# Equal blocks of nine neighbour chunks, and another order of the set-up, in a sparse four-layer graph network

## The chip, the cores and the metric

The kernel runs on one core of a Trainium2 chip. The metric is the device time of one execution in microseconds; lower is better. The engines named below are TensorE (PE; its weight loads are listed apart as PEld), VectorE (DVE), ScalarE (ACT), GpSimd (POOL) and SyncE (SP, which only issues DMAs). [...]

## The reference

Sixteen graphs with 1024 nodes of 128 features share one 1024 x 1024 adjacency matrix with about 8 edges per node. Four layers follow one another: graph transformer, graph attention, graph transformer, graph transformer.

```python
def _L0_gnn_ref(adj_matrix, h, Wq, Wk, Wv, Wo, bo, ln1_g, ln1_b, W1, b1, W2, b2, ln2_g, ln2_b):
    ...
    scores = jnp.einsum('bnhd,bmhd->bhnm', Q, K) / jnp.sqrt(jnp.asarray(HEAD_DIM, jnp.float32))
    mask = (adj_matrix == 0)[None, None, :, :]
    scores = jnp.where(mask, -jnp.inf, scores)
    attn = jax.nn.softmax(scores, axis=-1)
    attn_out = jnp.einsum('bhnm,bmhd->bnhd', attn, V).reshape(B, N, OUT_DIM)
    x = h + (attn_out @ Wo + bo)
    x = _layer_norm(x, ln1_g, ln1_b)
    y = jax.nn.relu(x @ W1 + b1) @ W2 + b2
    x = _layer_norm(x + y, ln2_g, ln2_b)
    return x

def _L1_gnn_ref(x, adj, W, a_src, a_dst, ln_gamma, ln_beta):
    h = x @ W
    e = (h @ a_src)[:, :, None] + (h @ a_dst)[:, None, :]
    e = jnp.where(e >= 0, e, NEG_SLOPE * e)
    e = jnp.where(adj[None, :, :] == 0, -jnp.inf, e)
    ...
    y = jnp.einsum('bij,bjd->bid', att, h) + x
```

Everything is fp32, with 8 heads of 16 features.

## The kernel before

Only existing edges are computed. The kernel sorts the nodes by degree, so that nodes with like numbers of neighbours stand together, and gathers each neighbour's key and value rows from a table in DRAM.

**Blocks and chunks.** The sorted nodes make eight rows of 128, each of four quarters of 32 nodes. A block of 128 nodes takes one quarter from each of four rows: `ROWS` (L55) says which, and `CAPS` (L61) how many neighbour slots each of the four quarters gets. Four slots of one quarter (4 x 32) fill one chunk of 128 gathered rows; the leftover slots of the four quarters share one mixed chunk. A chunk is one indirect DMA on POOL (L955). Before the change blocks have 11, 9, 9, 9, 9, 9, 9 and 7 chunks. `PIECES` (L92) puts chunks together in pairs, with the mixed chunk alone as the fourth piece, so a nine-chunk block has five pieces, an eleven-chunk one six, a seven-chunk one four. In an attention layer each piece is a part. In the graph attention layer, neighbouring pieces are merged to parts of up to four chunks.

**Order of units.** The 16 graphs form two groups of eight. A unit is one block of one group in one layer; units run layer by layer, group 0's eight blocks and then group 1's. For each part the main loop does: `products` on DVE (L967, gathered keys times queries), `exponentials` (a reduction on DVE, L990, and the exponential on ACT, L994), `weighted` on DVE (L1018, values times weights), then `summed` on PE (L1034, summing slots per node by 0/1 marks). When a unit's last part is summed, `divided` takes a reciprocal on DVE (L1071) and starts two tails, one for each half of the graphs: output projection, layer norms, feed-forward, and the next layer's projections to its table. Gathers run four parts ahead.

**What is put between.** After each of these steps `others()` issues a bit of the other work: pieces of the two tails ("a" and "b") and of the next unit's queries ("q"). In an attention layer it goes by a written list, `PLANS` (L834), of fifteen entries; a part has three openings for it, so five parts have fifteen. Where a block ends with entries still to do, the closing loop issues them at once (L1254). At the end of a unit all that is left in `fronts` is issued in a row (L1273).

**Set-up.** `graph` loads the adjacency matrix (`edges`, three buffers), counts degrees (L263), broadcasts a sort key through PE (`over_partitions`), ranks the nodes (L309), and turns ranks into node numbers (`node_i`, L366). Then it gathers the adjacency rows in sorted order (`by_position`, POOL) and makes for each row of 128 nodes the list of its neighbours, by repeated max-of-8 and match-replace passes on DVE (L402 to L410). A list as long as the row's largest cap, rounded up to 8, needs that many passes. `slots` spreads the lists to slots of a block: matmuls on PE, then `idx` and `marks` on DVE (L444 to L460). Beside it, `at_once(0)` projects group 0's input into the first table (PE L644, L573; ACT; table writes on SP). The generator `graph` yields numbers, which are steps of that projection to be issued, and words, on which the driver at L1169 issues other work: "load" for the first unit's input, "spread" and "slots" for the two halves of the first block's slots, "queries" for its queries. Group 1's input is projected by `at_leisure(1)` (the list `slow`) after the set-up, in steps between the parts of layer 0, and must be done before group 1's first gather.

Of the kernel before, what the change touches and what calls it, by code (L numbers as in the profile page):

```python
# [18 lines left out]
ALU = mybir.AluOpType  # L19
# [4 lines left out]
D = 128  # L24
# [19 lines left out]
T = N // P  # L44
# [7 lines left out]
S = 4  # L52
J = P // 32

ROWS = (  # L55
    (0, 1, 2, 3, 4, 5, 7, 6),
    (7, 6, 3, 5, 2, 1, 0, 4),
    (7, 6, 5, 1, 2, 0, 3, 4),
    (1, 0, 2, 3, 4, 7, 5, 6),
)  # L60
CAPS = (  # L61
    (24, 5, 4, 11), (12, 6, 6, 12), (10, 9, 8, 9), (9, 8, 11, 8),
    (8, 10, 10, 8), (7, 12, 13, 4), (5, 14, 9, 8), (6, 8, 8, 6),
)
TOP = max(map(max, CAPS))
QUADS = TOP // S
MIX = J


def row_of(t, j):  # L70
    return ROWS[j][t]
# [62 lines left out]
AHEAD = 4  # L134
# [11 lines left out]
def sparse_path(ctx: ExitStack, tc: tile.TileContext, a: dict, out: bass.AP, flag):  # L146


    nc = tc.nc
# [9 lines left out]
    ident = const.tile([P, P], F32, name="ident")  # L159
    make_identity(nc, ident)  # L160

    centre = const.tile([P, P], F32, name="centre")
    nc.vector.tensor_scalar(centre, ident, 1.0 / D, None, ALU.subtract)

    rep = const.tile([P, J, S, 32], F32, name="rep")
    nc.gpsimd.memset(rep, 0.0)
    for j in range(J):
        q = slice(32 * j, 32 * j + 32)
        nc.vector.tensor_copy(
            rep[q, j], ident[q, q].rearrange("p (o n) -> p o n", o=1).to_broadcast([32, S, 32])  # L170
        )

    def rep_of(j, whole=False):
        q = slice(0, P) if whole else slice(32 * j, 32 * j + 32)
# [41 lines left out]
    at = [0]  # L216
# [17 lines left out]
    def graph(wide):  # L234
# [54 lines left out]
        def over_partitions(col):  # L289

            ps = bank([T, P])
            nc.tensor.transpose(ps, col, ident)
            turn = s1.tile([T, P], F32, tag="turn", name="turn")
            nc.vector.tensor_copy(turn, ps)
            dst = accs.tile([P, HF, GH * D], F32, tag="acc", name="acc")
            dst = dst.rearrange("p h d -> p (h d)")
            for t in range(T):
                nc.tensor.matmul(
                    dst[:, t * P : (t + 1) * P], sel[:, t, :], turn, start=True, stop=True
                )  # L300
            return dst
# [2 lines left out]
        key = s1.tile([P, T], F32, name="key")  # L304
        nc.vector.scalar_tensor_tensor(key, deg, float(N), nid, ALU.mult, ALU.subtract)
        keys = over_partitions(key)
        rank = s1.tile([P, T], F32, name="rank")
        for t in range(T):
            nc.vector.tensor_scalar(  # L309
# [31 lines left out]
        for t in range(T):  # L341
# [13 lines left out]
            if t == 0:  # L355
                spread = over_partitions(pack)
# [17 lines left out]


        order = sorted({row_of(0, j) for j in range(J)})
        order += [q for q in range(T) if q not in order]
        ahead = [by_position(q) for q in order[:3]]
        there = s1.tile([P, T], F32, name="there")
        for j in range(J):  # L380
            rows = slice(32 * j, 32 * j + 32)
            for t in range(T):
                q = row_of(t, j)
# [13 lines left out]
        nc.vector.tensor_tensor(bad, bad, low, ALU.add)  # L397
        yield 2

        for at, q in enumerate(order):  # L400
            v = vs[:, :N]
            nc.vector.scalar_tensor_tensor(v, ahead[at], 0.0, values, ALU.not_equal, ALU.mult)  # L402
            if at + 3 < T:
                ahead.append(by_position(order[at + 3]))
            top = -(-max(SORTED_CAPS[q * J : (q + 1) * J]) // 8) * 8
            for k in range(0, top, 8):
                nc.vector.max(lists[:, q, k : k + 8], v)
                if k + 8 < top:
                    last, v = v, vs[:, N:] if k % 16 == 0 else vs[:, :N]
                    nc.vector.match_replace(v, lists[:, q, k : k + 8], last, 0.0)  # L410
                yield 1
            if 0 < at < 5:
                yield ("load", "spread", "queries", "slots")[at - 1]

    def slots():

# [367 lines left out]
    def at_leisure(g):  # L784
        def fetch(k):
            rows = ones_.tile([P, GH, D], F32, tag=("xg", "xh")[k % 2], name="xg")
            if k < T * HF:
                nc.sync.dma_start(
                    rows.rearrange("p g d -> p (g d)"),
                    a["x"][k // HF * P : (k // HF + 1) * P, columns(g, k % HF)],  # L790
                )
            return rows

        ahead = [fetch(0), fetch(1)]
        yield
        for k in range(T * HF):
            steps = natural(g, k // HF, k % HF, ahead.pop(0))
            held[0] = True
            next(steps)
            ahead.append(fetch(k + 2))  # L800
            yield
            yield from steps
            held[0] = False
            if wanted[0]:
                yield
# [59 lines left out]
    def loaded(u):  # L865

        if u >= len(units):
            return
        l, g, t = units[u]
        xs[units[u]] = inputs.tile([P, HF, GH, P], F32, tag="x", name="x")  # L870
        if l == 0:
            x = xs[units[u]]
            nc.gpsimd.indirect_dma_start(
                out=x.rearrange("p h g d -> p (h g d)"), out_offset=None,
                in_=a["x"].rearrange("n (k c) -> (n k) c", k=GR),
                in_offset=bass.IndirectOffsetOnAxis(ap=places[:, g, t : t + 1], axis=0),
            )
            for h in range(HF):
                yield "idle"
                yield "idle"  # L880
                yield
                turned(x[:, h], x[:, h])
            yield
            return
        nc.sync.dma_start(
            xs[units[u]].rearrange("p h g n -> p (h g n)"),
            kept[l, g][t].rearrange("p h c -> p (h c)"),
        )
# [203 lines left out]
    slow = []  # L1092
# [3 lines left out]
    def advance(gens):  # L1096
        for gen in list(gens):
            got = next(gen, "end")
            if got == "end":
                gens.remove(gen)  # L1100
            elif got == "free":
                free.append(gen)
# [58 lines left out]
    with tc.manual_schedule():  # L1161
        wide = [gather_buffer() for _ in range(EDGES)]
        setup, entry, weights = graph(wide), at_once(0), load_weights("L0")
# [2 lines left out]
        next(entry)  # L1166
        more = [weights, load_graph_weights()]
        rest = slots()
        for i, room in enumerate(setup):  # L1169
            if i == T:  # L1170
                for gen in more:
                    next(gen)
            if room == "load":
                for _ in loaded(0):
                    next(entry, None)
            elif room == "queries":
                for _ in entry:
                    pass
                for _ in queries(0):
                    pass  # L1180
            elif isinstance(room, str):
                next(rest)
            else:
                for _ in range(room):
                    next(entry, None)
        for _ in entry:
            pass
        scratch.close()
        prods = ctx.enter_context(tc.tile_pool(name="prods", bufs=4))
        smalls = ctx.enter_context(tc.tile_pool(name="smalls", bufs=3))  # L1190
        slow.append(at_leisure(1))
        second = loaded(1)
        next(second)
        for i in range(AHEAD - 1):
            gathered(i)
        nc.gpsimd.memset(wide[3], 0.0)
        gathered(AHEAD - 1)
        fronts.extend([islice(rest, WAIT + 2), second] + more)
# [519 lines left out]
```

## Time and profile before

| | us |
|---|---|
| median of 3 runs | 2179.24 (2172.41 to 2185.14) |
| the profiled execution, its own time | 2187.6 |
| its span in the profile | 2185.3 |
| DMA: bytes, mean rate | 636.09 MB, 291 GB/s |
| first table gather issued by POOL | 88.22 |
| first reciprocal that closes a block | 156.73 |
| last reciprocal that closes a block | 2144.77 |

The profile is that of one execution, so durations and the sums made from them are measured against 2187.6, not against the median. A row of the timeline gives the start, the busy time, engine, source line, operation and tiles, a count, and in brackets how long the engine had been idle and what ended the wait. A row of the stage table gives for a stretch of the span the busy time of each engine with the number of instructions, and then the clock granted to PE, the busy share of the DMA engines and their rate.

### The profile page before, as it was taken

How to read it: one execution, taken by the hardware profiler on the slowest of the kernel's cores; microseconds unless marked ns; L12 is line 12 of the kernel's file. 1: busy time of each engine (PE TensorE's matmuls, PEld its weight loads, DVE VectorE, ACT ScalarE, POOL GpSimd, SP SyncE). 2: the span in 40 equal slices, each digit the busy share in tenths (PEclk: the TensorE clock that was granted, in tenths of full speed). 3: DMA queues.
4: the chain of work that ended last, by engine and by line, in shares of the span. 5: the costliest groups of instructions: out<-in, count | busy, mean ns of one | idle time of the engine just before them, and what ended most of it. 6: DMA issues, size and time to landing. Idle time of an engine off the chain costs nothing.

```text
span 2185.3 us, 36956 instructions
## 1 busy us (share of the span) xinstructions
PE 1976.5 (90%) x13396; PEld 1245.4 (57%) x13396; DVE 1857.3 (85%) x1363; ACT 1524.6 (70%) x5041; POOL 1047.6 (48%) x699
## 2 busy tenths in 40 slices
PE   6689999999999989998999999999998899988986
PEld 5446666656655545554556655666655555555554
DVE  7897899699997566678999979999789898889993
ACT  3348888778887545555788786878867778677874
POOL 3343445354555577774445434444344545444540
PEclk8699999899999999999999999999999999999998
DMA  7898988789998799898998878999787878678860
GB/s 261 287 309 304 327 296 300 245 278 318 326 325 275 261 324 346 322 375 291 313 356 312 319 255 301 343 318 346 277 282 272 292 286 288 226 280 288 290 207 21
DMA packets 164703, 636.09 MB, mean 291 GB/s; under 512 B 34568, under 2 KB 37384, under 8 KB 116014
## 3 DMA queue, kind: packets, MB, share of 16 engines
q0 software_dynamic: 88720, 485.08, 62.1%
q1 hardware_dynamic: 75792, 148.57, 20.1%
q8 instruction: 107, 1.75, 0.3%
q14 instruction: 84, 0.69, 0.1%
HBM read 581.08 MB, written 92.34 MB: 308 GB/s over the span
## 4 chain that ended last, share of the span: by engine, by line
PE 55%; issue 15%; DVE 9%; ACT 8%; DMA 7%; POOL 5%; another core or an unknown queue 0%; POOLq 0%; DVEq 0%; ACTq 0%
PE acc L1034 13%; PE ps L644 6%; DMA e<-table,idx 6%; PE ps L728 6%; PE yps L742 6%; PE ps L919 5%; POOL e L955 4%; PE ps L573 4%; PE yps L718 3%; DVE pr L1018 3%; PE yps L717 3%; PE yps L746 3%; PE ps L910 2%; DVE pr L967 2%; DVE sc L990 2%
## 5 line engine op out<-in xcount | busy, mean ns | idle before, releaser
L955 POOL DMA_INDIRECT e<-table,idx x576 | 900.9, 1564 | 965.9 <-DVE pr L1018 757.4
L1018 DVE TENSOR_TENSOR pr<-e,ex 128x2048 f32<-128x2048 f32 (+1 forms) x320 | 662.0, 2078 | 68.3 <-ACT ex L994 45.4
L1034 PE MATMUL acc<-pr,marks 128*32 128x512 f32 x2624 | 506.0, 606 | 35.8 <-DVE o L1074 19.7
L967 DVE TENSOR_TENSOR pr<-e,qr 128x2048 f32<-128x2048 f32 x192 | 441.0, 2297 | 93.9 <-PE acc L1034 31.4
L990 DVE TENSOR_REDUCE sc<-pr 128x128 f32<-128x2048 f32 (+1 forms) x240 | 497.5, 2073 | 8.1
L621 ACT ACTIVATE z<-yps,root 128x128 f32<-128x128 f32 x888 | 313.2, 369 | 69.2 <-PE yps L746 46.1
L1034 PEld LDWEIGHTS acc<-pr,marks 128*32 128x32 f32 x2624 | 106.8, 110 | 292.1 <-issue 238.6
L742 PE MATMUL yps<-W,f 128*128 128x128 f32 x1520 | 253.2, 284 | 16.7 <-ACT f L737 16.7
L742 PEld LDWEIGHTS yps<-W,f 128*128 128x128 f32 x1520 | 203.3, 191 | 98.5 <-ACT f L737 59.4
L637 ACT ACTIVATE z<-yps,rstd 128x128 f32<-128x128 f32 x888 | 251.1, 367 | 1.6
L922 ACT COPY qr<-ps 128x512 f32<-128x512 f32 x384 | 203.3, 601 | 38.9 <-PE ps L919 35.4
L573 PE MATMUL ps<-Wkv,xT 128*128 128x256 f32 x768 | 202.8, 406 | 14.9 <-ACT xT L650 10.4
L577 ACT COPY kv<-ps 128x512 f32<-128x512 f32 x176 | 102.7, 589 | 158.6 <-PE ps L573 146.0
L737 ACT ACTIVATE f<-ps,b 128x512 f32<-128x512 f32 x190 | 130.3, 686 | 86.2 <-PE ps L728 83.9
L728 PE MATMUL ps<-x,W 128*128 128x512 f32 x384 | 186.7, 609 | 1.1 <-ACT x L652 1.1
L644 PE MATMUL ps<-ident,z 128*128 128x128 f32 x896 | 153.8, 286 | 37.5 <-ACT qr L922 17.7
L621 ACT ACTIVATION_READ_ACCUMULATOR z<-yps,root 128x1 f32 x888 | 185.8, 209 | 0.0
L573 PEld LDWEIGHTS ps<-Wkv,xT 128*128 128x128 f32 x768 | 144.0, 199 | 68.1 <-issue 15.6
L919 PE MATMUL ps<-q,rep 32*128 32x512 f32 x768 | 163.7, 681 | 19.5 <-ACT q L914 12.9
L644 PEld LDWEIGHTS ps<-ident,z 128*128 128x128 f32 x896 | 107.7, 142 | 88.2 <-ACT qr L922 40.0
L717 PE MATMUL yps<-Wo,oT 128*128 128x128 f32 x768 | 155.5, 285 | 2.6 <-issue 1.5
L718 PE MATMUL yps<-centre,x 128*128 128x128 f32 x768 | 154.5, 284 | 1.0 <-ACT x L713 0.2
(174 smaller groups left out, 2550.6 us busy)
## 6 DMA issues: line engine op xcount, KB each, us to landing
table<-kv SPq DMA_DIRECT2D x88, 512.0 KB
kept<-xT SPq DMA_DIRECT2D x96, 256.0 KB
x<-kept SPq DMA_DIRECT2D x48, 512.0 KB
qx<-qr SPq DMA_DIRECT2D x48, 256.0 KB
e<-table,idx POOLq DMA_INDIRECT x576
table<-kv SPq DMA_DIRECT2D x32, 256.0 KB
qx<-qr SPq DMA_DIRECT2D x18, 384.0 KB
qx<-qr SPq DMA_DIRECT2D x42, 128.0 KB
```

The lines of the kernel that those rows point to most:

```text
L573: nc.tensor.matmul(ps[:, k, :], x[:, i + k, :], w[LAYERS[l][0], "Wkv"], start=True, stop=True,)
L621: nc.scalar.activation(z[:, i, :], y[:, i, :], AF.Square, scale=D**-0.5, bias=root, accum_out=total[:, i : i + 1],)
L637: nc.scalar.activation(z[:, i, :], y[:, i, :], AF.Copy, scale=rstd[:, i : i + 1])
L644: nc.tensor.transpose(ps[:, i, :], z[:, i, :], ident)
L728: nc.tensor.matmul(ps, p["W1"][:, f * P : (f + 1) * P], x1.rearrange("p g n -> p (g n)"), start=True, stop=True,)
L742: nc.tensor.matmul(ps[:, i, :], f1[:, f, i * P : (i + 1) * P], p["W2"][:, f, :], start=(f == 0), stop=False,)
L919: nc.tensor.matmul(ps, rep_of(j), q[32 * j : 32 * j + 32], start=True, stop=True)
L955: nc.gpsimd.indirect_dma_start(out=es[i][:, k, :], out_offset=None, in_=tables[l, g][:, :], in_offset=bass.IndirectOffsetOnAxis(ap=idx[:, ...
L967: nc.vector.tensor_tensor(prs[i][0][:, :n, :], es[i][:, :n, :ROW], qx[u].rearrange("p (o c) -> p o c", o=1) if (MIX, 0) in piece else of_p ...
L990: nc.vector.tensor_reduce(sc[:, :n, :], prs[i][0][:, :n, :].rearrange("p k (a d) -> p k a d", d=HD), mybir.AxisListType.X, ALU.add,)
L1018: nc.vector.tensor_tensor(prs[i][k0 // 2][:, :m, :].rearrange("p k (a d) -> p k a d", d=d), es[i][:, k0 : k0 + m, base : base + ROW].rearr ...
L1034: nc.tensor.matmul(outs[32 * j : 32 * j + 32], marks[:, mark, :], rhss, start=(chunk == mine[0]), stop=(chunk == mine[-1]),)
```

## The change

The change gives every block 36 slots, and so nine chunks, by new tables `ROWS` and `CAPS`. The first block is made of sorted rows 1, 4 and 6, the row with the longest lists (row 0, 23 slots) goes to blocks 1, 4, 6 and 7. `TOP` is rounded up to a multiple of 8, which leaves it at 24.

In the set-up, the fill of `centre` and `rep` moves on DVE from the start to a function `constants()`, called after the sort key's broadcast. The order of words changes: the first unit's input gather is issued before the lists, the first half of the slots after the third list, the second half after the fourth list, followed by the first unit's input, its queries and the creation of `at_leisure(1)`; after the fifth list the first three parts' gathers and the second unit's input gather are issued. The projection of group 0 gets two steps for each max pass instead of one and is issued to its end before the first half of the slots. Where it has no step left, a step of `at_leisure(1)` is issued.

```diff
@@ -53,16 +53,16 @@
 ROWS = (
-    (0, 1, 2, 3, 4, 5, 7, 6),
-    (7, 6, 3, 5, 2, 1, 0, 4),
-    (7, 6, 5, 1, 2, 0, 3, 4),
-    (1, 0, 2, 3, 4, 7, 5, 6),
+    (1, 0, 2, 3, 4, 5, 6, 7),
+    (6, 7, 4, 3, 0, 5, 1, 2),
+    (4, 7, 3, 2, 5, 1, 6, 0),
+    (1, 7, 2, 3, 6, 4, 0, 5),
 )
 CAPS = (
-    (24, 5, 4, 11), (12, 6, 6, 12), (10, 9, 8, 9), (9, 8, 11, 8),
-    (8, 10, 10, 8), (7, 12, 13, 4), (5, 14, 9, 8), (6, 8, 8, 6),
+    (12, 6, 8, 10), (23, 5, 4, 4), (10, 8, 9, 9), (9, 9, 10, 8),
+    (8, 14, 8, 6), (9, 8, 11, 8), (6, 12, 6, 12), (5, 10, 13, 8),
 )
-TOP = max(map(max, CAPS))
+TOP = -(-max(map(max, CAPS)) // 8) * 8
@@ -160,15 +160,18 @@
     centre = const.tile([P, P], F32, name="centre")
-    nc.vector.tensor_scalar(centre, ident, 1.0 / D, None, ALU.subtract)
 
     rep = const.tile([P, J, S, 32], F32, name="rep")
     nc.gpsimd.memset(rep, 0.0)
-    for j in range(J):
-        q = slice(32 * j, 32 * j + 32)
-        nc.vector.tensor_copy(
-            rep[q, j], ident[q, q].rearrange("p (o n) -> p o n", o=1).to_broadcast([32, S, 32])
-        )
+
+    def constants():
+        nc.vector.tensor_scalar(centre, ident, 1.0 / D, None, ALU.subtract)
+        for j in range(J):
+            q = slice(32 * j, 32 * j + 32)
+            nc.vector.tensor_copy(
+                rep[q, j],
+                ident[q, q].rearrange("p (o n) -> p o n", o=1).to_broadcast([32, S, 32]),
+            )
@@ -304,6 +307,7 @@
         keys = over_partitions(key)
+        constants()
         rank = s1.tile([P, T], F32, name="rank")
@@ -374,6 +378,7 @@
         order = sorted({row_of(0, j) for j in range(J)})
+        heads = len(order)
         order += [q for q in range(T) if q not in order]
@@ -397,6 +402,7 @@
         yield 2
 
+        yield "load"
         for at, q in enumerate(order):
@@ -408,9 +414,13 @@
                     nc.vector.match_replace(v, lists[:, q, k : k + 8], last, 0.0)
-                yield 1
-            if 0 < at < 5:
-                yield ("load", "spread", "queries", "slots")[at - 1]
+                yield 2
+            if at == heads - 1:
+                yield "spread"
+            if at == heads:
+                yield "slots"
+            if at == max(heads, T - 4):
+                yield "gather"
@@ -1166,33 +1176,36 @@
         rest = slots()
+        first, second = loaded(0), loaded(1)
         for i, room in enumerate(setup):
             if i == T:
                 for gen in more:
                     next(gen)
             if room == "load":
-                for _ in loaded(0):
-                    next(entry, None)
-            elif room == "queries":
+                next(first)
+            elif room == "spread":
                 for _ in entry:
+                    pass
+                next(rest)
+            elif room == "slots":
+                next(rest)
+                for _ in first:
                     pass
                 for _ in queries(0):
                     pass
-            elif isinstance(room, str):
-                next(rest)
+                slow.append(at_leisure(1))
+            elif room == "gather":
+                for k in range(AHEAD - 1):
+                    gathered(k)
+                next(second)
             else:
                 for _ in range(room):
-                    next(entry, None)
-        for _ in entry:
-            pass
+                    if next(entry, "end") == "end":
+                        advance(slow)
+                        break
         scratch.close()
         prods = ctx.enter_context(tc.tile_pool(name="prods", bufs=4))
         smalls = ctx.enter_context(tc.tile_pool(name="smalls", bufs=3))
-        slow.append(at_leisure(1))
-        second = loaded(1)
-        next(second)
-        for i in range(AHEAD - 1):
-            gathered(i)
         nc.gpsimd.memset(wide[3], 0.0)
         gathered(AHEAD - 1)
```

## The prediction

> **What bounds the kernel now.** First read was the page, for the shares. TensorE (PE) carries the largest load; VectorE (DVE) follows; neither share says which of them a given stage waits for.
>
> ```profile
> PE 1976.5 (90%) x13396; PEld 1245.4 (57%) x13396; DVE 1857.3 (85%) x1363; ACT 1524.6 (70%) x5041; POOL 1047.6 (48%) x699
> ```
>
> Second, the span cut at the moments when DVE takes the reciprocal that closes a block (L1071): set-up up to the first product, first block, rest of layer 0 group 0, layer 0 group 1, then layer 1 with layer 2 group 0, layer 2 group 1, layer 3 group 0, layer 3 group 1, and the end.
>
> ```profile
> 0.00:99.30 99.30, 67.06 (x415) 52.55 (x415) 77.80 (x148) 35.79 (x62) 38.06 (x34) 0.79 0.78 266
> 99.30:156.70 57.40, 43.36 (x247) 24.35 (x247) 53.31 (x49) 20.69 (x43) 24.42 (x15) 0.88 0.90 317
> 156.70:415.50 258.80, 244.59 (x1890) 163.87 (x1891) 225.84 (x157) 209.11 (x701) 114.71 (x75) 0.99 0.87 305
> 415.50:693.10 277.60, 263.61 (x1801) 167.50 (x1800) 252.78 (x149) 217.30 (x768) 142.56 (x93) 0.98 0.85 295
> 693.10:1285.80 592.70, 542.83 (x3750) 329.91 (x3751) 469.71 (x412) 384.93 (x1357) 340.08 (x233) 0.99 0.90 320
> 1285.80:1567.70 281.90, 268.14 (x1774) 170.33 (x1773) 258.59 (x146) 221.26 (x704) 122.17 (x80) 0.99 0.87 310
> 1567.70:1859.00 291.30, 265.40 (x1729) 162.11 (x1728) 258.46 (x145) 215.03 (x694) 135.35 (x86) 0.96 0.81 281
> 1859.00:2144.80 285.80, 258.09 (x1668) 157.58 (x1667) 247.11 (x141) 206.16 (x672) 126.79 (x81) 0.95 0.70 246
> 2144.80:2185.30 40.50, 23.38 (x134) 17.16 (x132) 13.66 (x25) 14.29 (x47) 3.44 (x4) 0.79 0.08 29
> ```
>
> The columns are span, then busy time of PE, weight load, DVE, ACT, POOL, then granted clock, DMA share, GB/s. The reader should see that attention stages run with PE and DVE both near full, and that in each eight-block group some 20 to 30 us of DVE idle time is left.
>
> Third, where that idle time sits: DVE's timeline around one change of group (layer 3, block 7 of group 0 into block 0 of group 1).
>
> ```profile
> 1840.03 2.32 DVE L1018 TENSOR_TENSOR pr<-e,ex 128x2048 f32<-128x2048 f32 x1
> 1846.63 2.29 DVE L967 TENSOR_TENSOR pr<-e,qr 128x2048 f32<-128x2048 f32 x1 [4.28 <-PE ps L644]
> ...
> 1868.85 1.22 DVE L990 TENSOR_REDUCE sc<-pr 128x64 f32<-128x1024 f32 x1
> 1876.09 2.29 DVE L1018 TENSOR_TENSOR pr<-e,ex 128x2048 f32<-128x2048 f32 x1 [6.02 <-ACT ex L994]
> ```
>
> Two stalls, 4.28 and 6.02 us. The same pair is 5.5 and 10.8 us at the change inside layer 0, 5.4 and 7.2 inside layer 2, 5.4 and 5.5 from layer 2 to 3. Between reciprocals, normal nine-chunk blocks take 32.9 to 33.8 us in layer 0 group 1; the seven- and eleven-chunk pair at its start takes 31.15 + 51.55 = 82.7.
>
> Fourth, DVE's timeline of the set-up, for what the first product waits on.
>
> ```profile
> 1.92 10.73 DVE L169 COPY rep<-ident 32x128 f32<-32x128 f32 x4
> 17.35 1.22 DVE L263 TENSOR_SCALAR_CACHE_REDUCE e<-edges 128x1024 f32<-128x1024 int32 x1 [0.92 <-DMA edges<-in_adj]
> 28.88 1.22 DVE L263 TENSOR_SCALAR_CACHE_REDUCE e<-edges 128x1024 f32<-128x1024 int32 x1 [2.84 <-DMA edges<-in_adj]
> 35.04 1.28 DVE L309 TENSOR_SCALAR_CACHE_REDUCE e<-acc,key 128x1024 f32<-128x1024 f32 x1 [3.93 <-PE acc L298]
> 60.86 1.23 DVE L402 SCALAR_TENSOR_TENSOR e<-edges,e 128x1024 f32<-128x1024 int32 x1 [1.53 <-DMA edges<-in_adj,node_i]
> ...
> 99.34 2.29 DVE L967 TENSOR_TENSOR pr<-e,qr 128x2048 f32<-128x2048 f32 x1 [4.46 <-DMA e<-table,idx]
> ...
> 105.14 2.29 DVE L967 TENSOR_TENSOR pr<-e,qr 128x2048 f32<-128x2048 f32 x1 [1.19 <-DMA e<-table,idx]
> ```
>
> [...] four 32x128 copies beside POOL's memsets take 10.73 us, while the accumulating L263 runs its usual 1.22 us beside the same memsets. [...] Here the half clock appears just where the queries' matmuls wait for ACT: eight L919 matmuls take 4.82 us at 424.96 and 1.86 us at 351.92.
>
> **Part 1, constants later.** `centre` and `rep` leave the head of DVE's queue, where they hold it from 1.77 to 12.65, and come back after `over_partitions(key)`, into the 3.93 us wait before L309. With no POOL work there I take about 0.25 us each (the uncontended 128x128 copy wgT is 0.28), 1.2 us in all: hidden; without the wait they would cost 1.2. What is freed: the first L263 can run as soon as its edges land (estimate 5 us, three tiles of 0.5 MB at the 311 GB/s of that stretch), so edges 3 to 7, which SyncE issues only when a buffer comes free and ahead of other loads, go out up to 8 us earlier. The last L263 then waits for transfer and SyncE's order: table writes of the first projections (issued at 19.02 and 19.77, after ACT) stand before the last edges. I take its start at 24.5 instead of 28.88, so 4.4 us. Bounds: 0 if PE's queue (projections until 26.5) holds the transposition, 5.5 at best.
>
> **Part 2, order of lists, slots and gathers.** A pass over 1024 values is 1.25 us. Lists of 24, 16 and 8 cost 7.7, 5.0 and 2.5. Block 0 needs rows 1, 4, 6 (5.0 + 2.5 + 2.5) and one more list of 7.7 is put ahead of its slots (1.35). So its indices are ready 19.05 us after the lists begin, against 26.4 now (60.86 to 87.3). POOL has one more edge gather before them, which waits for the next list's first pass, so about 6 us are won. With part 1 the first table gather goes out near 78 instead of 88.22. It takes 11 us now, so it lands near 89. But all lists now cost 10 + 7.7 + 1.35 + 17.5 = 36.6 us (row 5 needs 16 places), so DVE is free only at 60.86 - 4.4 + 36.6 = 93. First product 93 instead of 99.34; the second at 97.6 instead of 105.14, its data landing by 95. Gain 7.5. SyncE and POOL: x of block 0 goes out before the lists, where POOL idles now; x of block 1 and its 0.5 MB fall behind the gathers. All projections of group 0 must be drained on PE before the slot matmuls; they end at 69.4 now but for eight matmuls held behind x (76.78). If they ended at 81 again, DVE would stand at the slots and the 7.5 would be 0.
>
> **Part 3, nine chunks everywhere.** Gathers stay 72 per group (44 + 6 x 36 + 28 = 8 x 36 slots) and parts 40. A pair of chunks costs DVE 2.29 + 2.29 + 2.28 = 6.8 us. Block 0 loses one pair: first block's end moves from 156.7 to 156.7 - 7.5 - 6.8 = 142.4, **-14.3**.
> Every attention block now has five parts, fifteen openings for the plan of tails and queries, whose list has fifteen entries. A seven-chunk block has twelve, so its last entries, "qqqqbbqq" and "ba" among them, run in one lump; that is the crowding behind both stalls. I take each boundary block at the mean of its group's middle blocks.
> Rest of layer 0 group 0, PE-bound: +1 for two more chunks, -3 for projections begun earlier (seven steps are two of sixteen projections, 2.5 us of PE each, less one lost with the shorter first block): **-2**.
> Layer 0 group 1: 8 x 33.2 = 265.6, against 277.6: **-12**.
> Layer 1 and layer 2 group 0: first graph block 36.0 to 31 (the work left over for PE), later ones conserved; last graph block +2.5, first attention block -6.7, block 7 +3: **-6**.
> Layer 2 group 1: 8 x 33.8 = 270.4 against 281.9: **-11.5**.
> Layer 3 group 0: 8 x 35.8 = 286.4 against 291.3: **-5**. Group 1: 7 x 35.6 + 33 = 282.2 against 285.8: **-3.5**. The last block grows by 7.4 here, and the end of 40.5 stays.
> Added: 83 marks for 82, and block 4 now has a pair in one 32-row column, whose four matmuls run one after another (0.43 us against 0.12 to 0.23 when columns differ): about 1 us of PE per group, mostly under DVE: **+2**.
>
> **Part 4, second group's projections in the set-up.** Cost nothing on PE (idle 2.4 of 5 us between 95 and 100). Their DMA, some 1 MB or 3 us, lies in the 4 us between landing and DVE's coming free; if that cover is gone, +3.
>
> Sum: -14.3 - 2 - 12 - 6 - 11.5 - 5 - 3.5 + 2 = **-52**. Own time of the profiled execution 2187.6 gives 2135; it lies 8.4 above the median of the runs shown, 2179.24, which gives **2127**.
>
> **Rivals.** (a) The stalls belong to the change of group, not to the seven and eleven chunks: for it, clock and stall coincide with first blocks; against it, the queries' lump comes from block 7's missing openings. Then the set-up's 14 and layer 1's 5 remain, less the longer last block's 7 and serial matmuls' 2: -10 to -17, 2165. Chance 0.13. (b) The set-up gives nothing, because PE's drain or SyncE's order hold it: 2135. Chance 0.15, inside the range. (c) Balanced blocks also lose the 1 to 2 us stalls of ordinary neighbours and layer 1 its half-clock stretches: -75, 2104. Chance 0.1. (d) Slower: the PE clock. PE is busier without lumps; mean clock is 0.964. At a mean of 0.91, PE's 1976 us grow by 117; with some 60% of the span PE-bound, +70 against -52 gives 2197. It decides from 0.915. [...] Chance 0.1.
>
> **Numbers.** Forecast 0.52. A measurement of this kernel tells about 0.5% (11 us) from no change. Faster: forecast, (b), (c) and most of (a), 0.83; same 0.08, from (a)'s upper end and part of (d); slower 0.09. The range 2100 to 2168 holds forecast, (b), (c) and most of (a).
>
> **What would show it.** First product near 93 and first reciprocal near 142; L263's first pass near 5 us and its last near 24.5; no DVE wait over 3 us in blocks 7 and 0 of attention layers; 33 to 36 us between their reciprocals; last block about 33. The prediction is wrong if 5 to 10 us stalls on `ex` remain at group changes, if DVE stands at the slots for PE, or if the clock falls outside the set-up.

## The result, and the profile after

The changed kernel takes 2143.77 us in the median of 6 runs (2143.00 to 2150.55), the kernel before beside it 2180.11 us (2170.12 to 2185.14, 6 runs). The ratio is 0.9867 with a 95% interval of 0.9846 to 0.9889. The profiled execution took 2143.22 us by its own time, with a span of 2141.5.

Two later measurements of the same changed program, on the two chips of the experiments, gave 0.9921 (0.9892 to 0.9950) and 0.9879 (0.9845 to 0.9913). The gain in these three measurements is therefore 14 to 36 us. Comparisons below are made within one chip where a few us matter. The profiled execution of the kernel before (2187.6) lies 7.5 us above its median, that of the changed kernel 0.6 below its own: the two profiles are 44 us apart where the medians are 36 apart, so differences between these two profiles come out somewhat large.

The page's first part, for the shares of the engines:

```profile
PE 1954.5 (91%) x13444; PEld 1237.4 (58%) x13444; DVE 1852.2 (86%) x1368; ACT 1522.8 (71%) x5043; POOL 1048.6 (49%) x699
```

The span is 43.8 us shorter. VectorE is busy for 5 us less than before, so most of what it gained is idle time. TensorE is busy for 22 us less although it has 48 more matmuls, so half of its gain is idle time and half is matmuls that took less time.

The stage table of the changed kernel, cut at its own reciprocals (the set-up and the first block are one row here). The columns are the span, then busy time and instructions of PE, weight load, DVE, ACT and POOL, then granted clock, DMA share and GB/s:

```profile
0.00:150.00 150.00, 104.95 (x663) 77.01 (x664) 117.19 (x196) 58.15 (x107) 54.77 (x46) 0.84 0.86 307
150.00:411.20 261.20, 249.88 (x1907) 165.45 (x1908) 232.57 (x160) 209.06 (x703) 118.67 (x77) 0.99 0.86 297
411.20:679.30 268.10, 256.99 (x1831) 164.81 (x1830) 253.05 (x148) 219.26 (x780) 141.11 (x91) 1.00 0.88 305
679.30:993.80 314.50, 284.94 (x2040) 168.95 (x2040) 211.28 (x262) 172.33 (x674) 209.67 (x155) 0.97 0.92 326
993.80:1270.20 276.40, 258.73 (x1700) 161.82 (x1698) 259.95 (x154) 209.93 (x668) 130.33 (x80) 0.99 0.90 316
1270.20:1546.30 276.10, 264.51 (x1780) 169.02 (x1779) 258.09 (x145) 220.91 (x704) 127.29 (x80) 1.00 0.89 317
1546.30:1826.70 280.40, 260.00 (x1736) 160.21 (x1734) 259.03 (x146) 214.73 (x693) 132.27 (x87) 0.98 0.82 293
1826.70:2101.60 274.90, 252.34 (x1672) 153.81 (x1673) 247.69 (x141) 206.34 (x675) 131.04 (x81) 0.97 0.73 255
2101.60:2141.50 39.90, 22.18 (x126) 16.32 (x125) 13.37 (x25) 12.13 (x41) 3.45 (x4) 0.78 0.08 29
```

The reader should compare stage by stage: from layer 0 group 1 on (third row) DVE's busy time is that of before within 2 us, while the spans of these stages shrank towards it. Only the second row, the rest of layer 0 group 0, grew, from 258.8 to 261.2.

VectorE's timeline of the set-up and of the first block, the rows that answer to those of before:

```profile
7.65 1.22 DVE L266 TENSOR_SCALAR_CACHE_REDUCE e<-edges 128x1024 f32<-128x1024 int32 x1 [6.73 <-POOL e L250]
...
24.67 1.22 DVE L266 TENSOR_SCALAR_CACHE_REDUCE e<-edges 128x1024 f32<-128x1024 int32 x1 [1.14 <-DMA edges<-in_adj]
...
27.21 0.91 DVE L171 COPY rep<-ident 32x128 f32<-32x128 f32 x4
29.36 1.28 DVE L313 TENSOR_SCALAR_CACHE_REDUCE e<-acc,key 128x1024 f32<-128x1024 f32 x1 [1.24 <-PE acc L301]
54.88 1.23 DVE L408 SCALAR_TENSOR_TENSOR e<-edges,e 128x1024 f32<-128x1024 int32 x1 [1.58 <-DMA edges<-in_adj,node_i]
...
90.91 2.27 DVE L977 TENSOR_TENSOR pr<-e,qr 128x2048 f32<-128x2048 f32 x1
95.42 2.28 DVE L977 TENSOR_TENSOR pr<-e,qr 128x2048 f32<-128x2048 f32 x1
...
135.14 2.29 DVE L977 TENSOR_TENSOR pr<-e,qr 128x2048 f32<-128x2048 f32 x1 [11.91 <-ACT qr L932]
...
150.03 0.56 DVE L1081 RECIPROCAL both<-ps 128x64 f32<-128x64 f32 x1
```

The first product starts 8.4 us earlier than before (90.91 for 99.34), the second 9.7 us earlier (95.42 for 105.14), and neither waits for its data. But the block's end is only 6.7 us earlier, though the block also lost a pair of chunks worth 6.8. A new wait of 11.91 us stands in between: the product at 135.14 is the first of the second unit, and its queries `qr` come late.

VectorE's timeline around the change of group in layer 3, the place that the prediction showed:

```profile
1791.48 0.55 DVE L1081 RECIPROCAL both<-ps 128x64 f32<-128x64 f32 x1
...
1819.92 2.29 DVE L977 TENSOR_TENSOR pr<-e,qr 128x2048 f32<-128x2048 f32 x1 [0.90 <-PE ps L654]
...
1826.65 0.55 DVE L1081 RECIPROCAL both<-ps 128x64 f32<-128x64 f32 x1
...
1842.09 2.29 DVE L977 TENSOR_TENSOR pr<-e,qr 128x2048 f32<-128x2048 f32 x1 [2.07 <-PE acc L1044]
...
1861.47 0.55 DVE L1081 RECIPROCAL both<-ps 128x64 f32<-128x64 f32 x1
```

The waits of 4.28 and 6.02 us are gone; what is left is 0.90 and 2.07. The two blocks take 35.2 and 34.8 us where they took 29.9 and 46.3, so 6.2 us are won. At the change in layer 0 the pair takes 32.91 and 33.03 (82.7 before, 65.9 after), and no DVE wait there is over 0.31 us.

### The profile page after: what moved, and what is told of

It reads as the page before. It is cut to its first block, busy times and chain, and to the rows that moved or that the text cites. A ratio compares the mean times of both kernels' runs of the same rounds, so it can differ in the third digit from the quotient of the medians.

```text
span 2141.5 us, 37070 instructions
## 1 busy us (share of the span) xinstructions
PE 1954.5 (91%) x13444; PEld 1237.4 (58%) x13444; DVE 1852.2 (86%) x1368; ACT 1522.8 (71%) x5043; POOL 1048.6 (49%) x699
## 4 chain that ended last, share of the span: by engine, by line
PE 68%; DVE 11%; ACT 8%; issue 6%; DMA 4%; POOL 2%; POOLq 0%; DVEq 0%; ACTq 0%
PE acc L1044 17%; PE yps L752 7%; PE ps L654 7%; PE ps L738 7%; PE ps L583 6%; PE ps L929 6%; PE yps L728 4%; PE yps L727 4%; DMA e<-table,idx 4%; PE yps L756 3%; DVE pr L1028 3%; PE ps L920 2%; DVE pr L977 2%; DVE sc L1000 2%; ACT qr L932 2%
## 5 line engine op out<-in xcount | busy, mean ns | idle before, releaser
L1044 PE MATMUL acc<-pr,marks 128*32 128x512 f32 x2656 | 516.1, 605 | 36.3 <-DVE pr L1028 18.3
L1000 DVE TENSOR_REDUCE sc<-pr 128x128 f32<-128x2048 f32 (+1 forms) x240 | 497.4, 2073 | 8.1
L583 PE MATMUL ps<-Wkv,xT 128*128 128x256 f32 x768 | 204.1, 409 | 12.7 <-ACT xT L660 5.5
L583 PEld LDWEIGHTS ps<-Wkv,xT 128*128 128x128 f32 x768 | 145.1, 201 | 67.5 <-issue 14.0
L654 PE MATMUL ps<-ident,z 128*128 128x128 f32 x896 | 148.9, 283 | 37.1 <-ACT qr L932 27.5
L929 PE MATMUL ps<-q,rep 32*128 32x512 f32 x768 | 146.7, 663 | 8.6 <-ACT q L924 7.6
L728 PE MATMUL yps<-centre,x 128*128 128x128 f32 x768 | 152.6, 281 | 0.5 <-ACT x L723 0.2
```

Source lines behind the costliest of these rows:

```text
L583: nc.tensor.matmul(ps[:, k, :], x[:, i + k, :], w[LAYERS[l][0], "Wkv"], start=True, stop=True,)
L654: nc.tensor.transpose(ps[:, i, :], z[:, i, :], ident)
L929: nc.tensor.matmul(ps, rep_of(j), q[32 * j : 32 * j + 32], start=True, stop=True)
L1000: nc.vector.tensor_reduce(sc[:, :n, :], prs[i][0][:, :n, :].rearrange("p k (a d) -> p k a d", d=HD), mybir.AxisListType.X, ALU.add,)
L1044: nc.tensor.matmul(outs[32 * j : 32 * j + 32], marks[:, mark, :], rhss, start=(chunk == mine[0]), stop=(chunk == mine[-1]),)
```

## The experiments

Two questions were open. Why does the set-up's lead of 8 us not reach the first block's end? And which part of the change carries the gain? The theories: the pieces stand alone, so that their gains add up; or they need each other. For the first block: the queries are late because they queue behind other work on TensorE and ScalarE; or TensorE simply has too much to do. Units are counted from 0, so the first reciprocal ends unit 0, and unit 7, group 0's last in layer 0, lies between the seventh and the eighth. Group 1's last projection (PE's last row on `xg`) is at 369.1 before and at 328.1 in the changed kernel. Experiments e1 to e8 ran on one chip, e9 to e12 on another.

### e1: the tables alone

```diff
 ROWS = (
-    (0, 1, 2, 3, 4, 5, 7, 6),
...
+    (1, 0, 2, 3, 4, 5, 6, 7),
...
-TOP = max(map(max, CAPS))
+TOP = -(-max(map(max, CAPS)) // 8) * 8
```

> Only the new ROWS and CAPS (nine chunks in every block) on the set-up of before. Theory A (the gain is the equal blocks; what the set-up won was lost again to the late queries of unit 1): 2145 to 2152 us, no DVE wait over 3 us at the changes of group, first product near 97 us and first closing reciprocal near 150 us. Rival B (the set-up carries more than half of the gain): 2160 us or more.

Measured: 2181.38 us (20 runs), ratio 0.9991 (0.9974 to 1.0008). The tables alone win nothing, and theory A missed: the first product is at 100.0, the first reciprocal at 154.7. Yet from the end of layer 0 to the last reciprocal this kernel takes 2143.3 - 706.3 = 1437.0 us, and the kernel before 2144.8 - 693.1 = 1451.7: around the group changes of layers 2 and 3 no DVE wait is over 2.0 us here. Layer 0 is 13 us longer than before. Its first block loses a pair of chunks worth 6.8 and yet ends only 2.0 us earlier, since DVE waits 5.10 us for the second unit's queries, and unit 7 takes 41.9 us where the changed kernel takes 32.9. Two views, the tile `xg` and DVE's timeline of unit 7:

```profile
L644 PE MATMUL ps<-ident,xg x64: 272/273/477, 98.0 to 400.9; 128*128 128x128 f32 x64
```

```profile
406.19 2.29 DVE L967 TENSOR_TENSOR pr<-e,qr 128x2048 f32<-128x2048 f32 x1 [4.45 <-PE acc L1034]
...
417.04 2.29 DVE L967 TENSOR_TENSOR pr<-e,qr 128x2048 f32<-128x2048 f32 x1 [5.10 <-DMA e<-table,idx]
```

Group 1's last projection comes at 400.9, in unit 7, and its table write is issued at 404.5. Group 1's first gather goes out at 408.6, 20 us after unit 6's reciprocal (9 us in the changed kernel), and DVE first waits for TensorE and then for that gather.

### e2: the set-up alone

```diff
 ROWS = (
-    (1, 0, 2, 3, 4, 5, 6, 7),
...
+    (0, 1, 2, 3, 4, 5, 7, 6),
...
```

This is the changed kernel with the old tables.

> The new set-up with the old ROWS and CAPS (11, 9 x 6, 7 chunks). Theory A: 2170 to 2178 us against 2180 before, with the stalls of 5 to 11 us at the changes of group as before, first product at 88 to 92 us. Rival B: 2160 us or less.

Measured: 2182.71 us (20 runs), ratio 1.0003 (0.9983 to 1.0023). The first product is at 91.17, 8.2 us earlier than before, and the first reciprocal at 156.75, against 156.73. DVE's timeline of the first block:

```profile
91.17 2.29 DVE L977 TENSOR_TENSOR pr<-e,qr 128x2048 f32<-128x2048 f32 x1 [0.87 <-DMA e<-table,idx]
...
141.88 2.29 DVE L977 TENSOR_TENSOR pr<-e,qr 128x2048 f32<-128x2048 f32 x1 [6.15 <-ACT qr L932]
...
156.75 0.56 DVE L1081 RECIPROCAL both<-ps 128x64 f32<-128x64 f32 x1
```

The row of the kernel before that answers to the second one has no wait:

```profile
141.86 2.29 DVE L967 TENSOR_TENSOR pr<-e,qr 128x2048 f32<-128x2048 f32 x1
```

The whole lead of the set-up is spent by waiting, most of it for the second unit's queries. And with the old tables the stalls at the changes of group are there as before, inside layer 2 for example:

```profile
1270.34 2.29 DVE L977 TENSOR_TENSOR pr<-e,qr 128x2048 f32<-128x2048 f32 x1 [4.68 <-PE ps L654]
...
1300.97 2.29 DVE L1028 TENSOR_TENSOR pr<-e,ex 128x2048 f32<-128x2048 f32 x1 [7.20 <-ACT ex L1004]
```

Layers 1 to 3 take 1455.6 us here and 1437.0 in e1 on the same chip.

So each half by itself is worth nothing (0.9991 and 1.0003), and together they are worth 14 us on this chip (e5).

### e3: the second unit's queries ahead of the weights

```diff
-        fronts.extend([islice(rest, WAIT + 2), second] + more)
+        fronts.extend([islice(rest, WAIT + 2), second, queries(1)] + more)
...
-                if u + 1 < len(units):
+                if 0 < u < len(units) - 1:
```

> The changed kernel, but in unit 0 the queries of unit 1 are issued ahead of the work on the weights. Theory A (unit 1's queries come too late because block 0 now has 15 openings for 18 or more steps): DVE's 11.9 us wait on qr falls below 4 us, first closing reciprocal 140 to 143 us, and 2134 to 2140 us in all. Rival C (layer 0 group 0 is bound by PE's total work from there on): the first reciprocal comes earlier, the eighth stays near 411 us, and 2142 to 2145 us in all.

Measured: 2162.41 us (4 runs), ratio 0.9896 (0.9843 to 0.9949). The wait for `qr` is gone, but DVE then waits 8.60 us at the prepared weights (L529, for a product of PE), and the first reciprocal is at 150.9. So the expected 140 to 143 was missed. The order of the queue only chose which of two late things DVE waits for, which points to something ahead of both.

### e4: the extra projection steps later

```diff
-                eager[0] = 1 if u < 2 else 0
+                eager[0] = 1 if 0 < u < 3 else 0
```

> The changed kernel, but the extra steps of group 1's projections that go with every opening are given in units 1 and 2 and not in units 0 and 1. Theory D (these projections' table writes hold the two kv buffers, so ACT and PE stand before unit 1's queries): the 11.9 us wait falls below 5 us, first closing reciprocal 139 to 145 us; in all 2135 to 2141 us if this is not paid back, 2143 to 2148 us if PE's work is only moved (rival C). Theory A alone: the wait stays above 8 us.

Measured: 2173.46 us (20 runs), ratio 0.9959 (0.9938 to 0.9979). Without the extra projection steps in unit 0 the wait for `qr` falls to 3.72 us and the first reciprocal comes at 142.0. But unit 2 now takes 47.8 us, the last projection comes at 393.8, and unit 7 takes 42.7. Without these steps the queries are not held up, but the projections have to be done by unit 7 all the same.

### e5: the changed kernel again

> The changed kernel itself once more, beside the others of this group. From layer 1 on, the tables-alone and queries-ahead kernels run the same sequence as it does and were yet 15 to 20 us slower over layers 1 to 3. Theory E (that spread comes with the chip or the execution): now 2155 to 2165 us. Theory F (it belongs to the program): 2143 to 2150 us as before.

Measured: 2167.66 us (5 runs, 2157.66 to 2170.57), ratio 0.9921 (0.9892 to 0.9950). The same program is 24 us slower than in its first measurement, with the kernel before at 2181.95. Most of what e3 and e4 seemed to lack in layers 1 to 3 belongs to this. By the medians e3 is 5 us below the changed kernel and e4 6 us above it, but the intervals of both overlap with this one, so neither is shown to differ from it.

### e6: no projections of group 1 in the set-up

```diff
-                slow.append(at_leisure(1))
...
-                    if next(entry, "end") == "end":
-                        advance(slow)
-                        break
+                    next(entry, None)
...
+        slow.append(at_leisure(1))
         nc.gpsimd.memset(wide[3], 0.0)
```

> The changed kernel without the steps of group 1's projections in the set-up: they begin behind it, as before. Theory G (with equal blocks the last of these projections is not done when group 1's first gather needs it, and is forced in unit 7): the closing reciprocal of unit 7 comes 40 to 43 us after that of unit 6 instead of 32.9, the last projection near 395 to 400 us, and the time is 8 to 14 us above the changed kernel's in this group. Theory A (nothing depends on it): within 3 us of it.

Measured: 2172.81 us (13 runs), ratio 0.9957 (0.9935 to 0.9978), so 5 us above e5; the intervals overlap a little. In the profile the first reciprocal is at 149.4, the last projection at 398.2, unit 7 takes 41.7, and the ninth reciprocal is at 464.0, where e5 has it at 449.0. DVE's timeline of unit 7 shows the pair of waits of e1 again:

```profile
403.50 2.29 DVE L977 TENSOR_TENSOR pr<-e,qr 128x2048 f32<-128x2048 f32 x1 [3.88 <-PE acc L1044]
...
414.67 2.29 DVE L977 TENSOR_TENSOR pr<-e,qr 128x2048 f32<-128x2048 f32 x1 [5.42 <-DMA e<-table,idx]
```

The few steps in the set-up decide whether the projections end before unit 7 or inside it. They are not what makes the queries late: without them the wait for `qr` is still 10.72 us.

### e7: the tables alone, with projection steps in three units

```diff
-                eager[0] = 1 if u < 2 else 0
+                eager[0] = 1 if u < 3 else 0
```

This edit is made to the kernel of e1.

> The equal blocks on the old set-up, as in the run with the tables alone, but the extra projection steps run for three units instead of two, so that they end by 350 us. Theory G: unit 7 falls from 41.9 to 33 to 34 us and unit 8 from 36 to 33 to 34, 8 to 14 us less than 2181: 2167 to 2173. Rival C (PE's total work binds layer 0 group 0 anyway): the eighth reciprocal stays near 430 and the time at 2178 to 2183.

Measured: 2174.01 us (6 runs), ratio 0.9970 (0.9953 to 0.9988). The last projection is at 308.7, and unit 7 takes 33.4 without a wait over 1 us. But unit 2 takes 44.2 us for e1's 36.9. The late projection of e1 is cured, and most of what it cost is paid elsewhere: the eighth reciprocal is at 428.1 for 430.5, and layer 0 ends 5 us before e1's.

### e8: the constants at the head again

```diff
-        constants()
...
+    constants()
```

> The changed kernel with the constants filled at the head of VectorE's queue again. Lists begin near 60.9 instead of 54.9 and the first product near 97 instead of 90.9. If the set-up's gain lives on to the end: 5 to 7 us above the changed kernel in this group. Rival C (layer 0 group 0 is bound by PE's work after the first block): 0 to 3 us above it.

Measured: 2168.34 us (4 runs), ratio 0.9936 (0.9914 to 0.9957). The first reciprocal is at 160.5, 7.8 us after e5's, and the end of layer 0 is 10.2 us after e5's; the time, however, is only 0.7 us above e5. Layers 1 to 3, with the same instructions, took 1426.8 us here and 1434.0 in e5. The loss is plain at the first block and within the scatter at the end.

### e9 to e12: the changed kernel, and two ways to free the second unit's queries

e9 is the changed kernel. e10 makes this edit to it:

```diff
             elif room == "gather":
+                next(second)
                 for k in range(AHEAD - 1):
                     gathered(k)
-                next(second)
```

e11 makes this one, and e12 both:

```diff
-                eager[0] = 1 if u < 2 else 0
+                eager[0] = 1 if 0 < u < 4 else 0
```

> The changed kernel once more, as the measure for the three that run beside it on the same chip. If the 20 us between its two earlier measurements belong to the place where it ran, it lands at 2160 to 2170 again, with the first reciprocal at 150 to 153 and the eighth at 411 to 416; if they were chance from run to run, it can land near 2144.

> The changed kernel with the second unit's input gathered ahead of the first three parts' gathers. If the 12 us wait of the first block's fourth product comes from that input being gathered late, its queries come some 8 us earlier, the wait falls below 5 us and the first reciprocal comes to 143 to 145, though the first product may start 2 to 4 us later. If ACT, held by key and value copies that wait for table writes, is what delays the queries, the wait stays at 8 us or more and the first reciprocal at 149 or later. Either way under 0.5% in the time.

> The changed kernel with the extra projection steps in units 1, 2 and 3 instead of 0 and 1. Theory one, a queue held by copies: without projection steps in unit 0 the first reciprocal comes at 142, and with three units of steps the projections end before unit 7, so that nothing runs in a lump and the eighth reciprocal comes 6 to 8 us before that of the changed kernel beside it, and the time 5 to 8 us below it. Theory two, TensorE's work sets the end of group 0's layer 0: the first reciprocal comes at 142, but the eighth within 3 us of the changed kernel's, and the time is the same.

> Both edits together. Theory one: first reciprocal at 138 to 141, eighth reciprocal 8 to 11 us before that of the changed kernel, time 6 to 11 us below it. Theory two: first reciprocal at 138 to 142, eighth within 3 us of the changed kernel's, time the same within 0.3%.

| | median us (6 runs) | ratio to before | first reciprocal | eighth | last |
|---|---|---|---|---|---|
| e9, the changed kernel | 2148.69 | 0.9879 (0.9845 to 0.9913) | 152.6 | 413.0 | 2101.4 |
| e10, input first | 2139.44 | 0.9839 (0.9807 to 0.9871) | 142.9 | 404.4 | 2093.9 |
| e11, steps in units 1 to 3 | 2154.66 | 0.9903 (0.9873 to 0.9934) | 142.2 | 417.8 | 2111.3 |
| e12, both | 2148.31 | 0.9878 (0.9838 to 0.9918) | 143.1 | 420.9 | 2105.4 |

e9 lies 5 us above the first measurement and 19 below e5. The expectation of e10 calls the product that waits the first block's fourth; it is the first of the second unit, as shown above.

How the second unit's input reaches its queries, in the changed kernel (its first trace, the timeline's rows of POOL, PE, ACT):

```profile
84.80 0.95 POOL L883 DMA_INDIRECT x<-in_x,places  x1 [0.30 <-issue]
...
100.62 1.09 PE L654 MATMUL ps<-ident,x 128*128 128x128 f32 x4 [4.14 <-DMA x<-in_x,places]
101.50 1.06 PE L654 MATMUL ps<-ident,xg 128*128 128x128 f32 x4
...
119.69 0.59 ACT L587 COPY kv<-ps 128x512 f32<-128x512 f32 x1 [7.72 <-DMA table<-kv]
...
120.33 2.07 PE L583 MATMUL ps<-Wkv,xT 128*128 128x256 f32 x4 [5.29 <-ACT kv L587]
...
127.27 1.07 ACT L932 COPY qr<-ps 128x512 f32<-128x512 f32 x2 [2.25 <-PE ps L929]
```

And in e10, with the same columns:

```profile
76.60 0.94 POOL L883 DMA_INDIRECT x<-in_x,places  x1 [0.30 <-issue]
...
96.38 0.60 PE L654 MATMUL ps<-ident,x 128*128 128x128 f32 x4
...
116.35 0.59 ACT L587 COPY kv<-ps 128x512 f32<-128x512 f32 x1 [1.35 <-PE ps L583]
...
120.57 1.07 ACT L932 COPY qr<-ps 128x512 f32<-128x512 f32 x2 [2.25 <-PE ps L929]
...
127.96 2.29 DVE L977 TENSOR_TENSOR pr<-e,qr 128x2048 f32<-128x2048 f32 x1 [4.42 <-ACT qr L932]
...
142.86 0.56 DVE L1081 RECIPROCAL both<-ps 128x64 f32<-128x64 f32 x1
```

In the changed kernel POOL issues the input behind six edge gathers; PE then stands for 4.14 us at its transposition, and the projection matmuls queued behind it run in a bunch from 101.5. Their copies on ACT use up the `kv` buffers, the next copy is held 7.72 us until a table write has landed (one was issued at 107.50; its counterpart in e10 at 105.09), PE waits for that copy (5.29 us at L583), and the query matmuls are behind. Nothing of ACT overtakes the held copy here: the exponential whose input DVE had finished at 114.40 (L1000, 1.21 us from 113.19) starts at 120.17, after it. This chain is read from the traces; no run gave `kv` more buffers. What the move does is shown by a run of its own. One issue moved past six takes the bunch away: DVE's wait falls from 12.44 us (e9) to 4.42 and the first reciprocal comes 9.7 us earlier. This lead is kept: 8.6 us at the eighth reciprocal, 9.1 at the sixteenth, 7.5 at the last. Five of e10's six runs lie below all of e9's; the two intervals overlap, from 0.9845 to 0.9871. e10 has the lowest ratio of the study: 1.6% below the kernel before, and by the medians 9 us below the changed one.

e11 shows the price of the other remedy. The first reciprocal comes at 142.2, but then the stage to the eighth is longer. The stage rows of e9 and of e11:

```profile
152.58:413.02 260.44, 249.09 (x1907) 164.74 (x1908) 232.53 (x161) 209.05 (x703) 118.58 (x77) 0.99 0.85 298
```

```profile
142.16:417.80 275.64, 263.75 (x1970) 176.42 (x1971) 232.63 (x161) 217.03 (x719) 113.81 (x77) 0.99 0.85 295
```

PE has 14.7 us more to do there, and the stage is 15.2 us longer, with the projections ended at 298.9. So TensorE's work is the bound in this stage, and the steps moved into it were paid in full. In unit 0 they cost nothing at the first block once the input comes first: 142.9 with them (e10), 143.1 without (e12). Both theories missed here: the eighth reciprocal is neither 6 to 8 us earlier nor within 3 us, but 4.8 later. In e12 the two remedies do not add up, since either one already frees the queries; its eighth reciprocal is 7.8 us later than e9's, which both theories missed too. At the last reciprocal 4.0 us of that are left, and the medians are the same.

## Why the prediction was right, and where its sum was not

The predicted median, 2127, is 17 us below the first measurement and inside the range. Between the medians 36 us were won where 52 were forecast. That the range would also have held e5's 2167.66, with its upper end at 2168, is luck. The prediction's steps against three profiles of the same or nearly the same program, each as a difference to the profile of before (the one that the prediction used; e9 and e10 ran on another chip than e1 to e8). That profile lies above its kernel's median, as said, and none of before was taken beside e9 and e10, whose medians lie 26 and 36 us below the kernel before. So the sums are larger than the gains, and differences of a few us between the columns say little:

| stage | predicted | changed, first | e9 | e10 |
|---|---|---|---|---|
| to the first reciprocal | -14.3 | -6.7 | -4.1 | -13.9 |
| rest of layer 0 group 0 | -2 | +2.4 | +1.6 | +2.7 |
| layer 0 group 1 | -12 | -9.5 | -9.5 | -9.9 |
| layer 1 and layer 2 group 0 | -6 | -1.8 | -9.7 | -8.4 |
| layer 2 group 1 | -11.5 | -5.8 | -5.9 | -5.1 |
| layer 3 group 0 | -5 | -10.9 | -10.2 | -7.8 |
| layer 3 group 1 | -3.5 | -10.9 | -5.6 | -8.4 |
| added | +2 | in the stages | | |
| end | 0 | -0.6 | +0.7 | +0.7 |
| sum | -52 | -43.8 | -42.7 | -50.1 |

**Part 1** was right in kind. The constants lie in the wait ahead of L313 and take 0.20 + 0.91 us there (1.2 predicted), the wait itself falling from 3.93 to 1.24; the last L266 starts at 24.67 (24.5 predicted). The same four copies took 10.73 us beside POOL's memsets and take 0.91 now, with POOL's memsets over since 19.5; with the constants at the head again (e8) they took 14.23. The first L266 was forecast at 5 us and starts at 7.65, held by POOL's own memset of `e` (L250), not by the edges. Undone alone (e8), this part costs 7.8 us at the first block, more than its 4.4.

**Part 2** was right in its mechanism and somewhat small in its size: 8.4 us at the first product instead of 6.3, and 9.7 at the second instead of 7.5. Beyond part 1, the first broadcast gave 1.7 us more: L301's sixteen matmuls took 2.02 us for 3.75. The granted clock was 0.50 during these matmuls before and is 1.00 now; during the eight L919 matmuls that the prediction compares it was 0.50 at 424.96 (4.82 us) and 1.00 at 351.92 (1.86 us). Ahead of the broadcast PE now comes from other matmuls, which end at 26.7; before it had stood idle for 4.02 us. That the idle time set the clock was not shown.

**The step that failed** is the one from there to the first block's end, "156.7 - 7.5 - 6.8 = 142.4". It assumed that what the front of the block gains reaches its end. The prediction named the cause and gave it no price: "x of block 1 and its 0.5 MB fall behind the gathers". That move costs 7 to 10 us: with the input put back ahead of the gathers (e10), everything else as in the change, the first reciprocal comes at 142.9, and without the extra projection steps in unit 0 (e4, e11) at 142.0 and 142.2. That e10 lands 0.5 us from the sum is in part luck, since a wait of 4.42 us is left there while its second product leads by 9.4 us instead of 7.5. The projection steps are the other half of the fault, and the prediction looked only at those in the set-up (part 4: "Cost nothing on PE"). PE's free time was there, but a copy of unit 0's projections waits 7.72 us for a `kv` buffer, until 119.69, and runs on ACT ahead of the queries' copies, which start at 127.27. The late input is not the only way to this wait: e1 has the old order of the set-up and a first block of nine chunks, and still waits 5.10 us for `qr`; e2 has the new order and eleven chunks and waits 6.15. In the changed kernel, with both, it is 11.91.

**Part 3 in layer 0 group 0** came near by two errors that cancel. "+1 for two more chunks, -3 for projections begun earlier" is, measured one at a time, about +17 (the stage is 275.8 us in e1, 258.8 before) and -15 (278.7 in e6, 263.2 in e5). Equal blocks push group 1's last projection from 369 to 401, into unit 7, and the set-up's steps bring it to 328. Why by as much as 32 us, the count of PE's rows on `xg` shows, four to a projection: up to the first reciprocal 8 of the 16 projections are begun before, 7 in e1 and e6, 9 in the changed kernel, then 3 in unit 1 and one in each later unit. The shorter first block has room for one projection less (the prediction's "less one"), and one less there moves the last one back by a whole unit. So the change's last part, counted as a small extra, is what lets the tables pay at all. That the stage came out within 5 us of the predicted -2 is luck.

**Part 3 in the later layers** was right in total: -26 predicted from layer 1 to the last reciprocal, -29.4 in the first profile. On the first chip of the experiments the seven profiles with new tables take 1427 to 1437 us there and the one with the old tables (e2) 1455.6, so 18 to 29 less. The predicted sign came: at the changes of group in the attention layers no DVE wait is over 2.07 us in the changed kernel. That equal blocks remove the stalls is shown by e1 and e2; that they do so because a seven-chunk block has too few openings for its list of entries was not tested apart from the sizes. The split over the stages was not right. Taking the boundary blocks at "the mean of its group's middle blocks" was good for the pairs (35.2 and 34.8 in layer 3, 33.3 and 34.3 in layer 2), but the middle blocks themselves moved: unit 41, behind the change of group in layer 2, went from 33.7 to 36.5, so layer 2 won half; those of layer 3 group 1 went from 35.65 to 34.97 in the mean and the last block grew by 4.8 instead of 7.4, so layer 3 won more than double.

**The rivals.** (a), that the stalls belong to the change of group, falls: with the same changes of group they are gone in layers 2 and 3 of every kernel with the new tables and there in e2. Those that e1, e4 and e6 show at the change inside layer 0 come with the late projections, for they are gone in e7 and in the changed kernel. The clock of (d) did not fall; the mean is 0.970 for 0.964. That a busier PE is granted a lower clock was the author's assumption and is not shown. (b) is near what happened at the first block, but not by PE's drain or SyncE's order: the set-up did give its 8 us, and the second unit's queries took them.

## What to carry to other kernels

A stall at a boundary can come from the boundary blocks' odd size alone; make blocks alike, then look at what else used their openings, because work that was done there is now due elsewhere and can come back as a stall at another boundary. A lead won at the front of a stage is worth what the next consumer's inputs allow: when a reordering moves a unit's gathers forward, price every issue that it puts behind them, above all the next unit's input. This was costly here, for the late input held not only its own work (4.14 us on TensorE) but the projections behind it, which ran from 101.5 on, and the bunch that followed ran out of buffers (7.72 us on ScalarE).

## What the runs showed of the hardware that had not been expected

The same changed program takes 2143.8, 2167.7 and 2148.7 us in three measurements, with the kernel before at 2180.1, 2182.0 and 2175.1 beside it, so the ratio of one measurement is not quite that of another. Chip and occasion are not separated here. In the profiles of the first two, DVE is busy for 1852.2 and 1852.1 us, PE for 1954.5 and 1970.7 with the same number of matmuls, at a mean clock of 0.970 and 0.967. Part of it is a lower granted clock in single blocks. The stage rows of the sixteenth block in the first trace and in e5:

```profile
647.30:679.30 32.00, 29.74 (x228) 19.52 (x226) 26.41 (x22) 23.38 (x95) 21.56 (x16) 1.00 0.88 275
```

```profile
654.30:689.20 34.90, 31.52 (x229) 21.30 (x227) 26.25 (x22) 23.42 (x95) 18.92 (x16) 0.95 0.87 274
```

A clock of 0.95 for 1.00, 1.8 us more of PE and a block 2.9 us longer. Layers 1 to 3 with identical instructions took from 1416.8 to 1437.4 us over the twelve profiles that have the new tables: 1422.3 in the first, 1426.8 to 1437.4 on the chip of e1 to e8 and 1416.8 to 1425.9 on that of e9 to e12. Why the granted clock of the same block differs between measurements was not found; it stays open.
